# A graph layer's opening on one core: a fourth block of raw rows, later small loads, other places for the stores of gathered blocks, and two operands in PSUM

## The chip, the core and the metric

The kernel runs on one core of one Trainium2 chip. The metric is the device time of one execution in microseconds (us); the three runs of the kernel before have a median of 4114.34 us (4112.78 to 4116.98). The core has five engines with a queue of instructions each: TensorE (PE in the profile, with weight loads as PEld), VectorE (DVE), ScalarE (ACT), GpSimd (POOL) and SyncE (SP). DMAs are issued from the queues of SP and ACT, and POOL issues indirect DMAs, which gather rows by a list of indices. All engines issue in order and wait for each other through semaphores.

## The reference, cut to what matters

There are N = 12500 nodes with C = 96 features, and E = 412500 edges, sorted by destination. Every edge has four attributes.

```
def mlp(h, W, b, gamma, beta):
    h = relu(h @ W + b)
    mu, var = mean(h, axis=0), mean(square(h - mu), axis=0)
    return gamma * (h - mu) * rsqrt(var + EPS) + beta

node_feat = mlp(x, W_node, ...)                     # N rows
edge_feat = mlp(edge_attr, W_edge, ...)             # E rows
message   = mlp(concat([x[src], x[dst], edge_feat]), W_msg, ...)
agg       = segment_sum(message, dst, N)
out       = layernorm(x + agg + node_feat)
```

The first 96 rows of W_msg act on x[src], the next 96 on x[dst]. So the kernel computes two tables once, p = x @ W_msg[:96] and q = x @ W_msg[96:192], and a message needs one row of p and one row of q. Norms are over all edges or nodes, so the statistics of edge_feat must be known before any message.

## The kernel before, in words

**Units.** 128 edges are a tile, 4 tiles a group (512 edges), 4 groups a block. There are 202 blocks and 3223 tiles. For every tile POOL issues one indirect DMA that fetches 128 rows of p (function `gather`, line L172); that is the only way in which p's rows reach the messages. q's rows need no gather, because edges are sorted by destination: a window of 31 rows serves a group.

**The opening, in the order of the code.** SP and ACT load x transposed (`xp`, seven pieces, L95) and the indices. `tables` (L157 to L165) computes p and q in seven chunks of 14 x 128 rows: matmuls, copies into one of two `trow` buffers, and per chunk one store to `p_tab` and one to `q_tab`, which alternate between SP and ACT. A third chunk cannot reuse a buffer before the first one's two stores have landed.

Main messages can start only after the edge statistics, but gathers need not wait. The first 26 blocks (`SPILL`) are gathered into one of two `stage` buffers and stored to DRAM (`spill`, L183) by SP; later they are read back. This is the generator `blocks`: each `next(store)` puts 16 gathers into POOL's queue and one store into SP's queue at that place of the code. A gather of block b needs the store of block b-2 to have landed, because there are two buffers. Blocks below `RAW` = 3 are gathered from x itself instead of p_tab, so they need not wait for the tables; the function `convert` (L435 to L443) multiplies them by W_msg[:96] when they come back in the main loop.

After the tables SP loads a few small things (L196 to L199), 13 pieces of the edge weights (`wide`, `we`, L202 to L207), and `dsti`, the destinations (L211). VectorE subtracts each block's first node (`basei`, L215) to get `rel`, and finds whether all edges fit their windows (`worst`, `flag`, L219 to L229). `places` (L235 to L252) loads the destinations in another layout (`lin`), subtracts `first` (L245), squares (L248) and stores both to DRAM (`rel_d`), two parts at a time. `lin` reuses the memory of `dsti`, and `dsti` that of `trow`. `nodes` (L261 to L284) computes the node features and stores them in 13 pieces (`y_d`, L282). `edge_norm` (L297 to L338) reads all edge attributes in 26 chunks of eight blocks (`ea`, two buffers), with matmuls, ReLU and batch statistics on VectorE (L309); between its chunks stand further `next(store)`, by a rule of 100 stores to 73 x the chunk's number.

**The main loop.** POOL gathers the 176 other blocks into a ring of 21 group buffers (`pg`). For a group PE makes z (L464), VectorE adds z and pg into hs (L475), ACT applies ReLU, PE sums (L497), VectorE accumulates (L510, L511). The 26 stored blocks are mixed evenly among the others. A short last part adds the node part and normalises the rows.

**What sets the order.** Inside `manual_schedule` SP and POOL keep the order of the code; a planner sorts everything else, by the time at which it thinks an instruction ready. The tables and their `next(store)` are one such section, `places` to `edge_norm` another. The small loads, the weights and `dsti` stood between them, so that the planner moved the loads forward among the stores of the tables.

Of the kernel before, what the change touches and what calls it, by code (L numbers as in the profile page):

```python
# [11 lines left out]
F32 = mybir.dt.float32  # L12
I32 = mybir.dt.int32
AF = mybir.ActivationFunctionType
OP = mybir.AluOpType
AX = mybir.AxisListType
ET = mybir.EngineType
PSUM = bass.MemoryType.PSUM
DRAM = bass.MemoryType.DRAM

N, C, E, ED = 12500, 96, 412500, 4
EPS = 1e-5
P = 128
# [3 lines left out]
GT, GE, BG = 4, 512, 4  # L27
NT = -(-E // P)
NG = -(-NT // GT)
NBL = -(-NG // BG)  # L30
NTP, NGP = NBL * BG * GT, NBL * BG
EP = NGP * GE
EK = ED + 1
Q = 32
NS = 3
RW = 7
# [14 lines left out]

SPILL = 26 * BG
RING = 21
RAW = 3
SKEW = 8
HB, RB = 2, 3
CL, CE = 2, 2
# [16 lines left out]
def gnn(ctx, tc, t):  # L74
    nc = tc.nc
# [31 lines left out]
    wide = const.tile([P, P], F32, name="wide")  # L107
    we = const.tile([P, C + WN], F32, name="we")


    step = const.tile([BG, 3, WN], F32, name="step")
# [13 lines left out]
    base = const.tile([1, NBL], I32, name="base")  # L125
    mstat = const.tile([C, 2], F32, name="mstat")
    vec = const.tile([C, len(_VECS)], F32, name="vec")
    v = {name[7:]: vec[:, i:i + 1] for i, name in enumerate(_VECS)}
    w_node = const.tile([C, C], F32, name="w_node")
    b_msg = const.tile([1, C], F32, name="b_msg")  # L130
# [56 lines left out]
    store = blocks()  # L187
    with tc.manual_schedule(engines={ET.SP, ET.Pool}):
        with tc.tile_pool(name="win_w", bufs=1) as work, tc.tile_pool(name="win_ps", bufs=4, space=PSUM) as ps:
            for i, _ in enumerate(tables(work, ps)):  # L190
                if i in (2, 4):
                    next(store)

    zero = const.tile([64, C], F32, name="zero")
    nc.vector.memset(zero, 0.0)
    nc.sync.dma_start(vec, t["vecs"])  # L196
    nc.sync.dma_start(w_node, t["L0_gnn_W_node"])
    nc.sync.dma_start(b_msg, t["L0_gnn_b_msg"])
    nc.sync.dma_start(base, t["base"])  # L199
    for i in range(NS):  # L200
        k, n = Q * i, C - Q * i
        nc.sync.dma_start(wide[k:k + EK, :n], t["wb"][:, C - n:])  # L202
        nc.sync.dma_start(wide[k + EK:k + 2 * EK, n:], t["wb"][:, :P - n])
    for i in range(BG):
        nc.sync.dma_start(we[Q * i:Q * i + EK, :C], t["wb"])
    for i in range(3):
        nc.sync.dma_start(we[ED + i:P:Q, C:], step[:, i, :])  # L207

    with tc.tile_pool(name="win", bufs=1) as win, tc.tile_pool(name="win_ps", bufs=2, space=PSUM) as ps:
        dsti = win.tile([P, NGP, GT], I32, name="dsti")  # L210
        nc.sync.dma_start(dsti, t["dst"].rearrange("p (g t) -> p g t", t=GT))  # L211
        basei = win.tile([P, NBL], I32, name="basei")
        nc.sync.dma_start(basei, t["base"].to_broadcast([P, NBL]))
        by_block = "p (b g) t -> p b (g t)"
        nc.vector.tensor_tensor(rel.rearrange(by_block, g=BG), dsti.rearrange(by_block, g=BG),  # L215
                                basei.unsqueeze(2).to_broadcast([P, NBL, BG * GT]), op=OP.subtract)
        worst = win.tile([P, 2, BG], F32, name="worst")
        for k in range(BG):
            nc.vector.tensor_reduce(worst[:, 0, k:k + 1], rel[:, k:NG:BG, :], axis=AX.XY, op=OP.max)  # L219
            nc.vector.tensor_reduce(worst[:, 1, k:k + 1], rel[:, k:NG:BG, :], axis=AX.XY, op=OP.min)  # L220
        out = win.tile([P, 1], F32, name="out")
        nc.vector.tensor_sub(worst[:, 0, :], worst[:, 0, :], iota[:, :, WN - 1])
        nc.vector.tensor_sub(worst[:, 1, :], iota[:, :, 0], worst[:, 1, :])
        nc.vector.tensor_reduce(out, worst.rearrange("p a k -> p (a k)"), axis=AX.X, op=OP.max)
        po = ps.tile([1, P], F32, name="po", bufs=1)
        nc.tensor.transpose(po, out, ident)
        most = win.tile([1, 1], F32, name="most")
        nc.vector.tensor_reduce(most, po, axis=AX.X, op=OP.max)
        nc.vector.tensor_scalar(flag, most, 0.0, None, op0=OP.is_gt)  # L229

    def places():

        with tc.tile_pool(name="lin", bufs=2) as work, tc.tile_pool(name="lin1", bufs=1) as one:
            first = one.tile([P, RW], I32, name="first")
            nc.sync.dma_start(first, t["first"])  # L235
            rows = [r.rearrange("o (p g e) -> (o p) g e", g=RW, e=GE) for r in rel_d]
            parts = [slice(i, min(i + 2, RW)) for i in range(0, RW, 2)]
            lins = []
            for i in range(len(parts) + 1):
                if i < len(parts):  # L240
                    n = parts[i].stop - parts[i].start
                    lins.append(work.tile([P, n, GE], I32, name="lin"))
                    nc.sync.dma_start(lins[i], t["dlin"][:, parts[i], :])
                    rlin = work.tile([P, n, GE], F32, name="rlin")
                    nc.vector.tensor_tensor(rlin, lins[i], first[:, parts[i]].unsqueeze(2).to_broadcast([P, n, GE]),  # L245
                                            op=OP.subtract)
                    square = work.tile([P, n, GE], F32, name="square")
                    nc.scalar.activation(square, rlin, AF.Square)  # L248
                    lins[i] = (rlin, square)
                if i:  # L250
                    for r, x in zip(rows, lins[i - 1]):
                        nc.sync.dma_start(r[:, parts[i - 1], :], x)  # L252

    def nodes():

        with tc.tile_pool(name="nd", bufs=1) as one, tc.tile_pool(name="nd_ps", bufs=2, space=PSUM) as ps:
            stats = one.tile([C, -(-N // GE), 6], F32, name="nstats")
            for i, c in enumerate(range(0, N, GE)):
                n = min(GE, N - c)
                pn = ps.tile([C, GE], F32, name="pn", bufs=4)  # L260
                nc.tensor.matmul(pn[:, :n], w_node, xp[:, c:c + n], start=True, stop=True)  # L261
                nc.scalar.activation(agg[:C, c:c + n], pn[:, :n], AF.Relu, bias=v["b_node"], scale=1.0)
                nc.vector.bn_stats(stats[:, i, :], agg[:C, c:c + n])
            aggr = one.tile([C, 2], F32, name="naggr")
            nc.vector.bn_aggr(aggr, stats.rearrange("p a b -> p (a b)"))
            a_n, c_n = norm(aggr, v["g_node"], v["beta_node"], "node")
            for c in range(0, N, N // 10):
                x, y = agg[:C, c:c + N // 10], xp[:, c:c + N // 10]
                nc.vector.scalar_tensor_tensor(y, x, a_n, y, op0=OP.mult, op1=OP.add)
                nc.scalar.activation(y, y, AF.Identity, bias=c_n, scale=1.0)  # L270
            for i in range(0, NB, NBY):
                n = min(NBY, NB - i)
                py = ps.tile([P, 2, GE], F32, name="py0")
                for g in range(n):
                    nc.tensor.matmul(py[:, g // NBK, g % NBK * C:(g % NBK + 1) * C],  # L275
                                     xp[:, (i + g) * P:(i + g + 1) * P], center, start=True, stop=True)
                y0 = one.tile([P, 2, NBK * C], F32, name="y0s", bufs=2)
                if n == NBY:
                    nc.vector.tensor_copy(y0, py[:, :, :NBK * C])
                else:  # L280
                    nc.vector.tensor_copy(y0[:, 0, :n * C], py[:, 0, :n * C])
                nc.sync.dma_start(y0_d[i // NBY][:, :n * C], y0.rearrange("p a b -> p (a b)")[:, :n * C])  # L282
                yield
            nc.vector.memset(agg, 0.0)  # L284
# [55 lines left out]
    def fast(ring):  # L340
# [3 lines left out]
        with tc.manual_schedule(engines={ET.SP, ET.Pool}):  # L344
            nc.sync.dma_start(q_tab[:WM, :], zero[:WM])
            for r in range(WM + NN, WT, 64):
                n = min(64, WT - r)
                nc.sync.dma_start(q_tab[r:r + n, :], zero[:n])
            next(store)
            places()  # L350
            next(store)
            next(store)
            for i, _ in enumerate(nodes()):
                if i in (1, 5, 10):
                    next(store)
            xpool.close()
            n = 0
            for i, _ in enumerate(edge_norm()):
                if 73 * i >= 50 + 100 * n:
                    next(store, None)  # L360
                    n += 1
            for _ in store:
                pass
            got = {g: ahead_of(g) for g in range(SPILL, SPILL + RING)}
# [11 lines left out]
        with tc.tile_pool(name="fix", bufs=1) as fix, tc.tile_pool(name="msg", bufs=2) as work, \  # L376
# [138 lines left out]
            n, ahead = len(steps), SPILL + RING  # L515
# [202 lines left out]
    with tc.tile_pool(name="fin", bufs=2) as work, tc.tile_pool(name="fin_ps", bufs=2, space=PSUM) as ps:  # L718
# [14 lines left out]
        for i in range(0, NB, NBY):  # L733
            n = min(NBY, NB - i)
# [55 lines left out]
```

## Time and profile before

| what | us |
|---|---|
| median of three runs | 4114.34 |
| profiled execution, its own time | 4124.01 |
| its span | 4122.3 |
| first gather starts | 3.15 |
| first gather of block 5 starts | 122.08 |
| first gather into the ring starts | 555.65 |
| first hs (main loop) starts | 633.54 |
| last gather starts | 4066.01 |
| POOL busy, 3244 instructions | 3072.2 |
| PE busy, mean granted clock 0.728 | 2875.0 |
| DVE busy | 1245.9 |

A line of a timeline gives the start and the duration in us, the engine (a q behind it: its queue issues, for a DMA), the line of the kernel, the operation, what it writes and reads, and in brackets how long the engine sat idle before and what ended that. A line of the waits gives the total in us, how many times, and the longest.

### The profile page before, as it was taken

The page shows a single profiled execution, that of the slowest core. Times are in us where ns is not written, and L with a number is a line of the kernel's source. Part 1 is how long each engine was busy: PE and PEld are TensorE (multiplying, and loading weights), DVE is VectorE, ACT ScalarE, POOL GpSimd, SP SyncE. Part 2 cuts the span into 40 slices and gives each one's busy share as a digit, 9 for nine tenths or more (in the row PEclk, how much of TensorE's full clock was granted, in tenths as well). Part 3 has the DMA queues.
Part 4 walks back from the last instruction along what each step waited for, and adds up shares of the span by engine and source line. Part 5 has one row for each costly group of instructions (what it writes and reads, how often), then busy time and mean ns, then how long its engine had stood idle before and what let it go on. Part 6 is the DMA issues. An engine that isn't in the chain of part 4 may idle for free. (4 is left out here: it accounts for less than half of the span.)

```text
span 4122.3 us, 46288 instructions
## 1 busy us (share of the span) xinstructions
PE 2875.0 (70%) x16517; PEld 2372.3 (58%) x16517; DVE 1245.9 (30%) x2410; ACT 1035.6 (25%) x804; POOL 3072.2 (75%) x3244
## 2 busy tenths in 40 slices
PE   4699968776667766666576667766777667666666
PEld 4455537666556655655565556666666556555555
DVE  2599983222122222222122212221222122221223
ACT  1387753221112211111122111121211122211112
POOL 6777777777777777777777777777777777777775
PEclk7655558877677778778777777776777677878777
DMA  8555532222222222222222222222222222222224
GB/s 241 170 115 110 106 78 67 48 54 54 53 53 47 54 52 47 53 55 54 52 47 54 52 54 46 54 55 52 46 54 54 53 46 54 54 52 47 54 53 114
DMA packets 190373, 274.29 MB, mean 67 GB/s; under 512 B 121571, under 2 KB 121956, under 8 KB 189126
## 3 DMA queue, kind: packets, MB, share of 16 engines
q0 software_dynamic: 103136, 158.62, 18.4%
q1 hardware_dynamic: 71684, 99.14, 8.8%
q10 hardware_dynamic: 15312, 13.47, 1.2%
q8 instruction: 133, 2.18, 0.2%
q14 instruction: 108, 0.88, 0.1%
HBM read 227.55 MB, written 43.43 MB: 66 GB/s over the span
## 5 line engine op out<-in xcount | busy, mean ns | idle before, releaser
L172 POOL DMA_INDIRECT pg<-p_tab,src x2807 | 2654.7, 946 | 856.9 <-issue 766.0
L464 PE MATMUL z<-rhs,left 128*128 128x96 f32 x6446 | 1172.6, 341 | 1050.8 <-issue 613.3
L464 PEld LDWEIGHTS z<-rhs,left 128*128 128x128 f32 x6446 | 1063.0, 250 | 1312.7 <-issue 718.6
L475 DVE TENSOR_TENSOR hs<-z,pg 128x384 f32<-128x384 f32 x702 | 391.4, 557 | 2510.5 <-DMA pg<-p_tab,src 2199.7
L497 PE MATMUL pa<-h 128*97 128x128 f32 x6446 | 1112.4, 330 | 12.5 <-ACT h L482 9.0
L497 PEld LDWEIGHTS pa<-h 128*97 128x97 f32 x6446 | 989.7, 212 | 18.5 <-ACT h L482 15.2
L482 ACT ACTIVATE h<-hs 128x1536 f32<-128x1536 f32 x201 | 298.1, 1483 | 2018.3 <-DVE hs L475 2018.3
L457 ACT ACTIVATE left<-pr 127x2048 f32<-127x2048 f32 x202 | 378.4, 1873 | 716.8 <-PE pr L450 716.8
L172 POOL DMA_INDIRECT stage<-p_tab,src x368 | 352.8, 959 | 127.9 <-issue 107.7
L303 PE MATMUL pr<-ea,wide 10*128 10x512 f32 x1212 | 372.0, 1062 | 18.8 <-DMA ea<-in_ea 18.8
L309 DVE BATCH_NORM_STATS2 estats<-r 128x6 f32<-128x512 f32 x606 | 361.3, 676 | 25.5 <-ACT r L307 25.5
L307 ACT ACTIVATE r<-pr 128x1024 f32<-128x1024 f32 x303 | 293.1, 1024 | 141.8 <-PE pr L303 117.9
L303 PEld LDWEIGHTS pr<-ea,wide 10*128 10x128 f32 x1212 | 198.2, 319 | 191.3 <-ACT r L307 85.3
L450 PE MATMUL pr<-ea,we 7*127 7x512 f32 x1404 | 229.6, 725 | 12.8 <-DMA ea<-rel_d 12.8
L478 DVE TENSOR_TENSOR h<-rel,z 128x496 f32<-128x496 f32 x202 | 133.4, 660 | 0.0
L511 DVE TENSOR_TENSOR gram<-pa,gram 97x388 f32<-97x388 f32 x202 | 111.3, 551 | 0.0
L510 DVE TENSOR_TENSOR agg<-pa,agg 97x62 f32 x404 | 90.0, 223 | 36.8 <-PE pa L497 20.8
L475 DVE TENSOR_TENSOR hs<-z,pb 128x384 f32<-128x384 f32 x104 | 57.7, 555 | 114.7 <-PE z L464 114.7
L450 PEld LDWEIGHTS pr<-ea,we 7*127 7x127 f32 x1404 | 61.4, 205 | 43.2 <-issue 23.4
L172 POOL DMA_INDIRECT stage<-in_x,src_raw x48 | 45.6, 949 | 27.3 <-issue 10.7
L275 PE MATMUL py<-center,xp 96*128 96x96 f32 x196 | 42.8, 423 | 31.5 <-ACT xp L270 18.5
L275 PEld LDWEIGHTS py<-center,xp 96*128 96x128 f32 x196 | 42.0, 332 | 32.3 <-ACT xp L270 18.9
(113 smaller groups left out, 501.4 us busy)
## 6 DMA issues: line engine op xcount, KB each, us to landing
pg<-p_tab,src POOLq DMA_INDIRECT x2807
spill<-stage SPq DMA_DIRECT2D x26, 768.0 KB
pb<-spill SPq DMA_DIRECT2D x26, 768.0 KB
ea<-in_ea SPq DMA_DIRECT2D x75, 160.0 KB
rhs<-q_tab SPq DMA_DIRECT2D x202, 46.5 KB
ea<-in_ea SPq DMA_DIRECT2D x352, 20.0 KB
stage<-p_tab,src POOLq DMA_INDIRECT x368
y_d<-y0s SPq DMA_DIRECT2D x12, 384.0 KB
```

The lines of the kernel that those rows point to most:

```text
L172: nc.gpsimd.indirect_dma_start(out=pg[:, i, :], out_offset=None, in_=tab[:, :], in_offset=bass.IndirectOffsetOnAxis(ap=idx[:, k:k + 1], ax ...
L303: nc.tensor.matmul(pr[:, k % 2, :], wide[Q * i:Q * i + 2 * EK, :], ea[Q * i:Q * i + 2 * EK, b % J, :], start=True, stop=True)
L307: nc.scalar.activation(r, pr, AF.Relu)
L309: nc.vector.bn_stats(stats[:, (k - o) % NS, (k - o) // NS, :], r[:, 1 - o, :])
L450: nc.tensor.matmul(prs[s][:C + WN, i, :], we[Q * i:Q * i + EK + 2, :], block[s][Q * i:Q * i + EK + 2, :], start=True, stop=True)
L457: nc.scalar.activation(x[:C + WN, :n, :], pr[:C + WN, :n, :], AF.Relu)
L464: nc.tensor.matmul(zs[k][:, i, :], left[s % 2][:KR, g % BG, i * P:(i + 1) * P], rhs[:KR, s % RB, g % BG, :], start=True, stop=True)
L475: nc.vector.tensor_add(hs[:, i, :n, :], z[:, :n, :], pg[:, :n, :])
L478: nc.vector.tensor_tensor(h[:, :, :, C + 1:C + 1 + WN], rel[:, b:b + BG, :].unsqueeze(3).to_broadcast([P, BG, GT, WN]), nodes_of.unsqueeze ...
L482: nc.scalar.activation(h[:, :, :, :C], hs, AF.Relu)
L497: nc.tensor.matmul(pas[s][:, g % BG, :C + 1 + WN], h[:r, i, :C + 1], h[:r, i, :C + 1 + WN], start=i == 0, stop=i == n - 1)
L511: nc.vector.tensor_add(gram[:, :n, :], pa[:, :n, :C + 1], gram[:, :n, :])
```

## The change

`RAW` becomes 4. In `tables` blocks 0, 1 and 2 are put behind chunks 0, 2 and 5 (before: blocks 0 and 1 behind chunks 2 and 4, block 2 ahead of `places`). Four small loads get a fixed place behind the tables; the 13 loads of edge weights become a function that is called behind `places` and two blocks. `nodes` has its three blocks behind stores 2, 5 and 11 (before 2, 6 and 11). The subtraction at L215 takes the blocks' first nodes from PSUM, spread over the partitions by a matmul with a row of ones, instead of from SBUF, spread by a DMA; `places` keeps a copy of `first` in PSUM.

```
-RAW = 3
+RAW = 4
...
             for i, _ in enumerate(tables(work, ps)):
-                if i in (2, 4):
+                if i in (0, 2, 5):
                     next(store)
+            nc.sync.dma_start(vec, t["vecs"])
+            nc.sync.dma_start(w_node, t["L0_gnn_W_node"])
+            nc.sync.dma_start(b_msg, t["L0_gnn_b_msg"])
+            nc.sync.dma_start(base, t["base"])
...
-    nc.sync.dma_start(vec, t["vecs"])
-    nc.sync.dma_start(w_node, t["L0_gnn_W_node"])
-    nc.sync.dma_start(b_msg, t["L0_gnn_b_msg"])
-    nc.sync.dma_start(base, t["base"])
-    for i in range(NS):
-        k, n = Q * i, C - Q * i
-        nc.sync.dma_start(wide[k:k + EK, :n], t["wb"][:, C - n:])
...
+    def edge_weights():
+        for i in range(NS):
+            k, n = Q * i, C - Q * i
+            nc.sync.dma_start(wide[k:k + EK, :n], t["wb"][:, C - n:])
+            nc.sync.dma_start(wide[k + EK:k + 2 * EK, n:], t["wb"][:, :P - n])
+        for i in range(BG):
+            nc.sync.dma_start(we[Q * i:Q * i + EK, :C], t["wb"])
+        for i in range(3):
+            nc.sync.dma_start(we[ED + i:P:Q, C:], step[:, i, :])
...
         nc.sync.dma_start(dsti, t["dst"].rearrange("p (g t) -> p g t", t=GT))
-        basei = win.tile([P, NBL], I32, name="basei")
-        nc.sync.dma_start(basei, t["base"].to_broadcast([P, NBL]))
+        ones = win.tile([1, P], F32, name="ones")
+        nc.vector.memset(ones, 1.0)
+        basef = win.tile([1, NBL], F32, name="basef")
+        nc.vector.tensor_copy(basef, base)
+        pb = ps.tile([P, NBL], F32, name="pb", bufs=1)
+        nc.tensor.matmul(pb, ones, basef, start=True, stop=True)
...
-                                basei.unsqueeze(2).to_broadcast([P, NBL, BG * GT]), op=OP.subtract)
+                                pb.unsqueeze(2).to_broadcast([P, NBL, BG * GT]), op=OP.subtract)
...
-            first = one.tile([P, RW], I32, name="first")
-            nc.sync.dma_start(first, t["first"])
+            firsti = one.tile([P, RW], I32, name="firsti")
+            nc.sync.dma_start(firsti, t["first"])
+            first = ps.tile([P, RW], F32, name="first")
+            nc.vector.tensor_copy(first, firsti)
...
-            next(store)
             places()
             next(store)
             next(store)
+            edge_weights()
+            next(store)
             for i, _ in enumerate(nodes()):
-                if i in (1, 5, 10):
+                if i in (1, 4, 10):
                     next(store)
```

More of the change, by code (lines that the diff above doesn't have):

```diff
@@ L190, in gnn @@
             for i, _ in enumerate(tables(work, ps)):
-                if i in (2, 4):
+                if i in (0, 2, 5):
                     next(store)
+            nc.sync.dma_start(vec, t["vecs"])
+            nc.sync.dma_start(w_node, t["L0_gnn_W_node"])
+            nc.sync.dma_start(b_msg, t["L0_gnn_b_msg"])
+            nc.sync.dma_start(base, t["base"])
     zero = const.tile([64, C], F32, name="zero")
     nc.vector.memset(zero, 0.0)
-    nc.sync.dma_start(vec, t["vecs"])
-    nc.sync.dma_start(w_node, t["L0_gnn_W_node"])
-    nc.sync.dma_start(b_msg, t["L0_gnn_b_msg"])
-    nc.sync.dma_start(base, t["base"])
-    for i in range(NS):
-        k, n = Q * i, C - Q * i
-        nc.sync.dma_start(wide[k:k + EK, :n], t["wb"][:, C - n:])
[L203 to L207, printed above, removed]
+    def edge_weights():
[7 more added lines that the diff above has]
+            nc.sync.dma_start(we[ED + i:P:Q, C:], step[:, i, :])
     with tc.tile_pool(name="win", bufs=1) as win, tc.tile_pool(name="win_ps", bufs=2, space=PSUM) as ps:
@@ L231, in places @@
     def places():
-        with tc.tile_pool(name="lin", bufs=2) as work, tc.tile_pool(name="lin1", bufs=1) as one:
-            first = one.tile([P, RW], I32, name="first")
-            nc.sync.dma_start(first, t["first"])
+        with tc.tile_pool(name="lin", bufs=2) as work, tc.tile_pool(name="lin1", bufs=1) as one, \
+                tc.tile_pool(name="lin_ps", bufs=1, space=PSUM) as ps:
+            firsti = one.tile([P, RW], I32, name="firsti")
+            nc.sync.dma_start(firsti, t["first"])
+            first = ps.tile([P, RW], F32, name="first")
+            nc.vector.tensor_copy(first, firsti)
             rows = [r.rearrange("o (p g e) -> (o p) g e", g=RW, e=GE) for r in rel_d]
```

## Prediction

> **What bounds the kernel now.** I read the page first, then the waits of GpSimd, then the timelines of GpSimd and SyncE over the opening, and last the start of the main loop. The page's chain was no help: it reaches back only to 4077 us. The page's span, its engine row and the costliest group:
>
> ```profile
> span 4122.3 us, 46288 instructions
> PE 2875.0 (70%) x16517; PEld 2372.3 (58%) x16517; DVE 1245.9 (30%) x2410; ACT 1035.6 (25%) x804; POOL 3072.2 (75%) x3244
> L172 POOL DMA_INDIRECT pg<-p_tab,src x2807 | 2654.7, 946 | 856.9 <-issue 766.0
> ```
>
> POOL looks 75% busy, but between two gathers lie 0.30 us that the profile calls issue. The waits of POOL say how often it waited for something else:
>
> ```profile
> POOL pg L172 <- issue: 766.0, 2512, 0.3
> POOL pg L172 <- DMA pg<-p_tab,src: 82.1, 266, 1.3
> POOL stage L172 <- DMA spill<-stage: 9.7, 3, 5.6
> ```
>
> 766.0 over 2512 is 0.30 each, so a gather costs 0.95 + 0.30 = 1.25 us and POOL runs flat out. All 3223 take 4029 us. The first starts at 3.15 and the last at 4066.01, 4062.9 apart, so everything that ever held POOL adds up to some 35 us. That is the most that any change outside the gathers can win. From POOL's timeline (start, duration, line, and in brackets the idle time before), the holds of the opening:
>
> ```profile
> 24.50 0.95 POOL L172 DMA_INDIRECT stage<-in_x,src_raw  x1 [0.84 <-DMA stage<-in_x,src_raw]
> 54.91 0.94 POOL L172 DMA_INDIRECT stage<-in_x,src_raw  x1 [5.65 <-DMA spill<-stage]
> 75.85 0.95 POOL L172 DMA_INDIRECT stage<-p_tab,src  x1 [1.25 <-issue]
> 85.86 3.18 POOL L172 DMA_INDIRECT stage<-p_tab,src  x1 [0.30 <-issue]
> 122.08 0.95 POOL L172 DMA_INDIRECT stage<-p_tab,src  x1 [3.75 <-DMA spill<-stage]
> 555.65 0.95 POOL L172 DMA_INDIRECT pg<-p_tab,src  x1 [0.30 <-issue]
> ```
>
> 122.08 is gather 80, the first of block 5. Flat out from 3.15 it would start at 103.15; 18.9 us were lost, about 6.4 of them between 15 and 32 us (a gather waits for one eight earlier, beside the loads of xp), 5.35 at 54.91 (block 2 waits for block 0's store), 0.95 at 75.85 (p_tab), 2.2 at 85.86, 0.5 near 102, 3.45 at 122.08 (block 5 waits for block 3's store). SyncE's timeline shows why these stores are late:
>
> ```profile
> 34.05 0.40 SPq L165 DMA_DIRECT2D p_tab<-trow  x1
> 43.84 2.55 SPq L183 DMA_DIRECT2D spill<-stage  x1
> 55.20 2.66 SPq L183 DMA_DIRECT2D spill<-stage  x1
> 68.90 0.36 SPq L165 DMA_DIRECT2D p_tab<-trow  x1
> 76.02 0.36 SPq L211 DMA_DIRECT2D dsti<-in_dst  x1
> 97.12 0.81 SPq L243 DMA_DIRECT2D lin<-in_dlin  x2
> 116.44 0.32 SPq L252 DMA_DIRECT2D rel_d<-square  x1
> 117.06 4.96 SPq L183 DMA_DIRECT2D spill<-stage  x2
> ```
>
> Block 3's store stands behind places(), whose last store goes at 116.44. places() in turn stands behind the flag, that behind dsti, and that behind the last rows of the tables. This chain on SP is what I follow.
>
> **The change, part by part.** The sum is against the profiled execution (4124.01 us, span 4122.3), which is 9.7 us above the median of 4114.34; I carry differences over to the median.
>
> *Small loads moved* (13 of edge weights, 4 others). In front they made table stores wait: ScalarE's copy at 34.06 was held 12.41 us by "DMA wide<-in_wb", and the first p_tab store went at 34.05 though its last copy ended at 18.7. Now it can go at about 19. Yet SP meets block 0's store next and waits for its gathers (last one issued at 24.50, landed by 33). So block 0's store goes at some 34 instead of 43.84, and lands by 34 + 11 = 45 (old: 43.84 to 54.91). Block 2 wants the buffer at 49.6: the 5.35 us go, and gathers 32 to 47 run 5.35 us sooner, the last issued at 73.66 - 5.35 = 68.3. Behind places() the 13 loads cost SP 13 x 0.3 to 2.5 us (the rows of L202 to L207) before block 5's store, whose gathers need until about 143 anyway: hidden; uncovered, 4 to 30 us on SP.
>
> The Trainium skill's "DMA: Bandwidth & Descriptors", section "Queues, rings and completion order", has each engine consume one queue's ring in order; by it the store issued at 19 moves nothing until the xp loads ahead of it land near 31, so these 15 us of issue would be worth some 4. No part of my sum uses them.
>
> *Fourth raw block.* Gathers 48 to 63 read x, so block 3 waits for no p_tab: 0.95 us gone. A raw gather costs 949 ns against 946: nothing. Its convert in the main loop is one more of three (L435 to L443: 15 us of PE in the row at 650.6 to 665.2), and hidden, because VectorE there waits 2199.7 us for pg. Uncovered it is 15 us, once.
>
> *PSUM operands.* L215 (3.53 us from 84.69) and the L245 operations (1.23 us) stretch gathers beside them: 3.18 and 1.41 us instead of 0.95. The copy to `first`, the memset, the basef copy and one K=1 matmul are about 0.2 us each by VectorE's small rows, 0.4 by po's matmul (L226). Whether a PSUM operand frees POOL no row shows: bounds 0 and 2.7 us. The Trainium skill's "SBUF — State Buffer", section "Who interferes with whom", says two SBUF inputs contend with a GpSimd operation that reads SBUF and one does not, which would give the 2.7 us; it also infers that such operations spare descriptor writing, which the 3.18 us row contradicts. In the sum this is worth 0, because POOL now waits further on. `first` also takes a bank of PSUM until the last L245 (115.6 us), and may keep the nodes' matmuls (from 96.93) waiting.
>
> *The wait that collects all this.* Block 5 needs block 3's buffer. Gathers 48 to 79 would now be done 12.5 us sooner, block 5 wanting to start at 109.6. But its release follows SP's chain, and there block 2's store now stands ahead of the last p_tab store, and four small loads behind it:
> - block 2's gathers landed: 68.3 + 4.3 to 6.9 (block 4: 117.38 to 121.7; block 1: 48.32 to 55.2), I take 73.0;
> - p_tab's last store behind that 0.79 MB store: 5.0 to 7.1 us (117.06 to 122.08 for one such store; 68.90 to 76.02 for the two last table stores), I take 5.9, so 78.9 against 76.0 before; the four loads and the zero rows fit inside it;
> - dsti until L215: 8.67 before, with basei (0.43 us of issue) and a zero store behind it; 7.0 to 8.7, I take 7.4, so 86.3 against 84.69;
> - L215 to block 5: 122.08 - 84.69 = 37.4, less 0.9 for eight gathers fewer beside the places' 6 MB (0 to 1.5): 36.5.
>
> Block 5 starts at 122.8: **0.7 us later than before**, with all ends together 120.5 to 128.4. The holds that vanish at 54.91, 75.85, 85.86 and 102 come back as one wait of about 13 us. From there on POOL's order is unchanged.
>
> *Stores at other places.* Block 6 after y_d 2, 7 after y_d 5, 8 after y_d 11. Block 8's gathers land near 206, so y_d 12 and 13 and the first ea loads go at about 207 instead of 196 and 197, and in edge_norm every ea chunk now stands behind the store of the block after the one before. At its end three chunks instead of two follow the last gathered block (557.04): 24 x 0.594 = 14.3 us more VectorE (L309), so the main loop starts some 15 us later relative to POOL. What covers it: 21 buffers are 84 gathers, filled at 555.65 + 105 = 660.7, while the first hs was at 633.54: 27 us, of which 12 remain.
>
> Sum: +0.7, so 4114.34 + 0.7 = **4115.0 us**.
>
> **The rivals.**
> 1. *The new wait is short.* If places() ended by 104, block 5 would start at 109.6: -12.5, time 4101.8; half of it, 4108. For it: dsti needs only the c6 rows landed, and SP is less crowded. Against it: block 2 cannot land before 72.6, so SP's own order allows block 5 no earlier than 120.5.
> 2. *Slower: the ring fills before the main loop starts.* Place: the 85th pg gather. From 27 us of delay on, every us costs one. 15 are used; if PSUM's bank keeps the nodes' stage from 96.93 to 117 (20 us), and the stores do not hide it, the delay is 35: +8 to +9, time 4123. Against: y_d 12 waits for block 8's gathers anyway, which hides about 10 of the 20.
> 3. *SP held, no more.* SP waits for block 0 and 1 while later table rows stand ready, c5 and c6 slip, and all takes its late end: block 5 at 128.4, +6.3, time 4120.6.
>
> **How the numbers follow.** A difference under 0.2% (8.2 us) is what a measurement of this kernel can hardly tell from none. Chances: forecast 0.68, rival 1 0.13, rival 2 0.11, rival 3 0.08. Rival 1 mostly goes below 4106 (0.10), with tails of the forecast, whose later holds on the ea loads may shift by 3 us: faster 0.12; rival 2 and the tails of rival 3: slower 0.10; the rest, 0.78, the same. The range reaches from half-way into rival 1, 4105, to rival 2's price, 4123; forecast alone 4110 to 4120.
>
> **What would show it.** After: one wait of 10 to 16 us ahead of the first gather of block 5 for "spill<-stage", none at block 2; that gather at 120 to 128; p_tab's first store near 19; no gather of 3 us beside L215; the first hs some 15 us later; pg still waiting on issue only. Wrong if block 5 starts before 114, or pg gathers wait for hs.

## The result, and the profile after

The changed kernel takes 4121.01 us (median of 22 runs, 4116.90 to 4124.89). The kernel before, on the same chip, takes 4113.72 us (22 runs, 4109.92 to 4117.26). The ratio is 1.0017 with a 95% interval of 1.0011 to 1.0023: some 7 us more, inside the 0.2% that I called no change, though the interval's upper end reaches past it. The forecast was 4115.0, so 6 us are missing from it.

The profiled executions hide this. They took 4124.01 us before and 4123.96 after, because that of before lay 9.7 us above its median, and POOL's pace differs: from the first ring gather to the last, 2806 gathers later, it is 1.2510 us per gather before and 1.2483 after ((4066.01 - 555.65) / 2806 and (4065.09 - 562.40) / 2806), 7.7 us over the whole. No run shows the kernel to be the cause of those 7.7 us: the four edited kernels on an equal chip, below, lie between at 1.2496 to 1.2502, and the difference is there ahead of the ring too, where unheld gathers (numbers 110 to 416) follow each other at 1.2509 and 1.2484. So I take times from medians and only places and waits from the profiles.

The page after, its span, engine row and costliest group:

```profile
span 4122.2 us, 46400 instructions
PE 2811.1 (68%) x16567; PEld 2316.5 (56%) x16567; DVE 1251.1 (30%) x2417; ACT 1038.0 (25%) x808; POOL 3063.1 (74%) x3244
L172 POOL DMA_INDIRECT pg<-p_tab,src x2807 | 2648.4, 944 | 855.5 <-issue 789.7
```

The bound is the same: one gather after the other, 0.94 + 0.30 us. So everything is again decided by what holds POOL, and the waits of POOL after (total, times, longest) say what that is:

```profile
POOL pg L172 <- DMA pg<-p_tab,src: 59.1, 194, 0.3
POOL stage L172 <- DMA stage<-p_tab,src: 22.1, 19, 3.7
POOL stage L172 <- DMA spill<-stage: 12.8, 1, 12.8
```

Waits of 0.3 us are the ordinary gap between two gathers under another name. The last two rows are real. Three waits for a store of gathered blocks (9.7 us before) have become one of 12.8. And the waits for an earlier gather's landing have grown from 16.2 us in 16 waits to 22.1 in 19, the longest from 2.4 to 3.7. POOL's timeline after (start, duration, in brackets the idle time before) shows the places:

```profile
49.74 0.94 POOL L172 DMA_INDIRECT stage<-in_x,src_raw  x1 [0.30 <-issue]
87.19 0.94 POOL L172 DMA_INDIRECT stage<-in_x,src_raw  x1 [0.30 <-issue]
89.69 0.95 POOL L172 DMA_INDIRECT stage<-p_tab,src  x1 [0.30 <-issue]
108.41 0.94 POOL L172 DMA_INDIRECT stage<-p_tab,src  x1 [0.30 <-issue]
122.13 0.94 POOL L172 DMA_INDIRECT stage<-p_tab,src  x1 [12.78 <-DMA spill<-stage]
363.53 0.94 POOL L172 DMA_INDIRECT stage<-p_tab,src  x1 [1.28 <-DMA stage<-p_tab,src]
370.63 0.94 POOL L172 DMA_INDIRECT stage<-p_tab,src  x1 [3.66 <-DMA stage<-p_tab,src]
562.40 0.94 POOL L172 DMA_INDIRECT pg<-p_tab,src  x1 [0.30 <-issue]
```

Block 2 (49.74) waits for nothing, nor does the first gather from p_tab (89.69), and the gather at 87.19, beside the subtraction L221 (L215 of before), takes 0.94 us and not 3.18. All that was won stands at 108.41, the last gather of block 4, and all of it goes in the wait that follows: block 5 starts at 122.13, against 122.08 before. The two rows near 365 are the other kind of wait. By gather number, the time lost against 1.2503 us per gather (a pace between those of the two profiles) is:

| gathers | before | after |
|---|---|---|
| 0 to 80 | 18.9 | 19.0 |
| 80 to 208 | 3.9 | 5.3 |
| 208 to 416 | 9.5 | 14.9 |
| first ring gather (number 416) starts | 555.65 | 562.40 |

So in these two profiles the opening costs the same, and the difference of 6.75 us arises behind it, nearly all of it while the edge attributes are read. SyncE's timeline after, first the chain that I followed:

```profile
22.77 0.40 SPq L165 DMA_DIRECT2D p_tab<-trow  x1
33.16 0.33 SPq L183 DMA_DIRECT2D spill<-stage  x1
71.55 0.33 SPq L183 DMA_DIRECT2D spill<-stage  x1
71.99 0.83 SPq L165 DMA_DIRECT2D p_tab<-trow  x1
79.76 0.36 SPq L213 DMA_DIRECT2D dsti<-in_dst  x1
116.22 0.32 SPq L261 DMA_DIRECT2D rel_d<-square  x1
116.84 1.49 SPq L183 DMA_DIRECT2D spill<-stage  x2
```

and then a place where gathers were held, from the same view, with the answering place of before in a second fence:

```profile
351.46 0.35 SPq L183 DMA_DIRECT2D spill<-stage  x1
351.98 5.39 SPq L306 DMA_DIRECT2D ea<-in_ea  x6
```

```profile
370.27 0.35 SPq L183 DMA_DIRECT2D spill<-stage  x1
370.78 11.47 SPq L297 DMA_DIRECT2D ea<-in_ea  x6
```

After, the six loads of two chunks (160 KB each) go out within 5.39 us, right behind a store of 0.79 MB. Gathers issued just behind them land late, and a gather waits for the one eight earlier: that of 370.63 waited for the one issued at 356.32, which so took some 14 us to land. Before, at 370.78, the six take 11.47 us, and POOL loses 0.2 us behind them. Of the pairs of chunks in edge_norm, five go out within 5.4 to 6.9 us after, three before. The short ones are followed by 2.2 to 4.3 us of holds each, the three of 9.5 to 11.5 us by 0.2 to 0.6, and the first pair of before, 13.59 us long, by 1.4. A single chunk right behind a store is followed by 0 to 0.8 us, and one that goes over 1 us behind it by none. That is the suspicion, theory A, that the experiments had to test.

### The profile page after: what moved, and what is told of

Its sections match the earlier page's. It is cut to its first block, busy times and chain, and to the rows that moved or that the text cites. A ratio compares the mean times of both kernels' runs of the same rounds, so it can differ in the third digit from the quotient of the medians.

```text
span 4122.2 us, 46400 instructions
## 1 busy us (share of the span) xinstructions
PE 2811.1 (68%) x16567; PEld 2316.5 (56%) x16567; DVE 1251.1 (30%) x2417; ACT 1038.0 (25%) x808; POOL 3063.1 (74%) x3244
## 5 line engine op out<-in xcount | busy, mean ns | idle before, releaser
L172 POOL DMA_INDIRECT pg<-p_tab,src x2807 | 2648.4, 944 | 855.5 <-issue 789.7
L474 PE MATMUL z<-rhs,left 128*128 128x96 f32 x6446 | 1122.8, 331 | 1093.1 <-issue 650.2
L474 PEld LDWEIGHTS z<-rhs,left 128*128 128x128 f32 x6446 | 1016.2, 240 | 1349.5 <-issue 763.4
L507 PE MATMUL pa<-h 128*97 128x128 f32 x6446 | 1085.7, 324 | 16.1 <-ACT h L492 13.3
L507 PEld LDWEIGHTS pa<-h 128*97 128x97 f32 x6446 | 960.9, 207 | 23.5 <-ACT h L492 20.1
L172 POOL DMA_INDIRECT stage<-p_tab,src x352 | 335.1, 952 | 137.6 <-issue 102.7
L312 PEld LDWEIGHTS pr<-ea,wide 10*128 10x128 f32 x1212 | 207.4, 320 | 193.7 <-issue 88.3
L172 POOL DMA_INDIRECT stage<-in_x,src_raw x64 | 60.5, 946 | 27.1 <-issue 16.2
L157 PE MATMUL pt<-w_msg,xp 96*128 96x192 f32 x196 | 41.9, 384 | 27.8 <-DVE trow L163 18.4
```

Source lines behind the costliest of these rows:

```text
L172: nc.gpsimd.indirect_dma_start(out=pg[:, i, :], out_offset=None, in_=tab[:, :], in_offset=bass.IndirectOffsetOnAxis(ap=idx[:, k:k + 1], ax ...
L312: nc.tensor.matmul(pr[:, k % 2, :], wide[Q * i:Q * i + 2 * EK, :], ea[Q * i:Q * i + 2 * EK, b % J, :], start=True, stop=True)
L474: nc.tensor.matmul(zs[k][:, i, :], left[s % 2][:KR, g % BG, i * P:(i + 1) * P], rhs[:KR, s % RB, g % BG, :], start=True, stop=True)
L507: nc.tensor.matmul(pas[s][:, g % BG, :C + 1 + WN], h[:r, i, :C + 1], h[:r, i, :C + 1 + WN], start=i == 0, stop=i == n - 1)
```

## The experiments

Theory A: the 7 us come from the place of the gathered blocks' stores in edge_norm. Because nine blocks instead of eight are issued before it, each chunk of edge attributes stands behind the store of one block later; SP then finds both `ea` buffers empty more often, sends two chunks back to back, and they hold the gathers. Theory B: the loss is in the opening (the one long wait), or spread, and the place in edge_norm is worth nothing. The first four runs were on a chip where the kernel before takes 4116.68 us. The changed kernel itself was not run there, so it is compared with them by its ratio to the kernel before, 1.0017.

**e1: the rule of edge_norm shifted back by one block, in the changed kernel.**

```
-            n = 0
+            n = 1
```

> The changed kernel, but in edge_norm every gathered block's store goes one step of the rule later (n starts at 1 instead of 0), so that ea chunks stand behind the same blocks' stores as before the change. Theory A (the 7 us were lost in edge_norm, where two chunks' loads now go back to back behind a store and late gathers hold POOL): the holds of POOL from the first ea load to the first ring gather fall from 15 to about 9.5 us, the first hs is some 12 us earlier, time 4114 to 4116. Theory B (they were lost earlier, by the nodes' stage that now starts 18 us later, or by the wait at block 5): time 4120 to 4122.

Measured: 4113.87 us (4111.87 to 4115.62), ratio to the kernel before 0.9993 (0.9984 to 1.0002). Its timeline of SP at the same place:

```profile
368.57 0.35 SPq L183 DMA_DIRECT2D spill<-stage  x1
370.03 15.26 SPq L306 DMA_DIRECT2D ea<-in_ea  x6
```

The six loads now take 15.26 us, since SP waits for a buffer between the two chunks, and no gather behind them is held. The time lost in gathers 208 to 416 falls from 14.9 to 1.0 us, the waits for earlier gathers from 22.1 to 6.2, and the ring starts at 547.44 instead of 562.40. Block 5 still starts at 120.83. The holds fall further than the 9.5 us that I expected by theory A. This one number takes back the whole loss, and theory B falls.

**e2: block 3's store ahead of places(), in the changed kernel; the rule as changed.**

```
+            next(store)
             places()
             next(store)
-            next(store)
             edge_weights()
```

> The changed kernel, but block 3's store stands on SyncE ahead of places() instead of behind it. My account of the change (everything that vanished from POOL's opening came back as one wait of 12.5 us at block 5, for this store): the wait is gone, block 5 starts at about 109.7 instead of 122.1, and all of it reaches the end: time about 4108.5. Rival (another wait takes its place within the next blocks, since their stores stand behind places and the nodes): block 5 early, but 4118 or more.

Measured: 4107.49 us (4105.89 to 4111.22), ratio 0.9980 (0.9970 to 0.9989). SP and POOL of this kernel:

```profile
78.55 0.36 SPq L213 DMA_DIRECT2D dsti<-in_dst  x1
89.63 0.36 SPq L183 DMA_DIRECT2D spill<-stage  x1
97.75 0.81 SPq L252 DMA_DIRECT2D lin<-in_dlin  x2
```

```profile
107.13 0.95 POOL L172 DMA_INDIRECT stage<-p_tab,src  x1 [0.30 <-issue]
108.38 0.94 POOL L172 DMA_INDIRECT stage<-p_tab,src  x1 [0.30 <-issue]
```

108.38 is the first gather of block 5, and it waits for nothing. The store goes at 89.63, while SP would only have waited for the places' first operands. The opening now loses 5.3 us instead of 19.0, and the kernel is some 16 us below the changed one (1.0017 x 4116.68 = 4123.7, less 4107.5). So the gains that the change made in the opening were real, and were lost to the order of two lines of code. They are not all of the 16 us: the ring starts 20.8 us sooner (541.61), of which 13.7 come from the opening and 7.1 from fewer holds behind it, because only three pairs of chunks go out within 5.9 to 6.4 us here, with the rule of the changed kernel. 10.4 us in gathers 208 to 416 remain.

**e3: both edits, in the changed kernel.**

```
+            next(store)
             places()
             next(store)
-            next(store)
             edge_weights()
...
-            n = 0
+            n = 1
```

> Both edits together, block 3's store ahead of places() and edge_norm's stores one step later. If the two losses are separate they add: 4121 - 12.5 - 6 = about 4102.5, which is under both kernels. If they share a cause (a POOL that is earlier finds the ea loads earlier too and is held longer): 4106 to 4110.

Measured: 4103.65 us (4102.53 to 4108.71), ratio 0.9970 (0.9961 to 0.9981). This beats both kernels.

```profile
108.02 0.94 POOL L172 DMA_INDIRECT stage<-p_tab,src  x1 [0.30 <-issue]
537.73 0.94 POOL L172 DMA_INDIRECT pg<-p_tab,src  x1 [0.30 <-issue]
```

The opening loses 4.9 us, gathers 208 to 416 lose 0.1. The ring starts 24.7 us sooner than in the changed kernel. What is left is 9.5 us in gathers 80 to 208, of which 6.7 lie at three gathers between 216.9 and 237.6. The first two of them (4.6 us) fit the same pattern: the very first six loads of edge attributes find both buffers empty and go out from 202.57 to 205.02. That was not tried apart.

**e4: the rule shifted the other way in the kernel before.** If theory A holds, this alone must make the kernel before slower.

```
-            n = 0
+            n = -1
```

> The kernel before, with only edge_norm's stores one step earlier (n starts at -1), which is where the change puts them; all else as before. Theory A: the loss of the change shows without the change, holds up by 4 to 6 us, first hs some 12 us later, time 4118 to 4120. Theory B: no difference, 4113 to 4115.

Measured: 4120.83 us (4117.96 to 4122.83), ratio 1.0010 (1.0001 to 1.0019), so 4 us slower, and at the lower end of the interval nothing. Gathers 80 to 208 lose 5.8 us (3.9 before), 208 to 416 lose 10.5 (9.5). SP's timeline shows the pattern of the changed kernel: five pairs of chunks go out within 5.9 to 6.7 us, where the kernel before has three, and each is followed by 2.4 to 2.7 us of holds. The sign is as theory A has it; the size is less than the 10 us by which e1 moved the changed kernel, and the two profiles alone show only 1 us of it at the start of the ring (556.70 against 555.65, the latter from an execution 9.7 us above its kernel's median).

So e1 and e4 show that the place of the stores in edge_norm changes how long gathers are held. That it does so through the two chunks sent back to back is read from the six profiles: ahead of the ring's start all 16 pairs that go out within 5.4 to 6.9 us are followed by 2.2 to 4.3 us of holds, and the 18 that take 9.5 to 16.2 us by at most 1.5 (those of e1 and e3 by at most 0.4, also where, as at 328.18 and 428.60 in e1, they stand right behind a store). The run made to test the loads by themselves, e8, decides nothing.

**The other eight runs** were made to price the parts of the change singly. They came to chips on which TensorE at times stands still for over 20 us, and the kernel before takes 5300 to 5314 us; so they answer a different question from the one that was asked, and only comparisons among themselves are used. This is the changed kernel there (run e11), TensorE's timeline:

```profile
37.77 9.25 PE L157 MATMUL pt<-w_msg,xp 96*128 96x192 f32 x36 [11.10 <-DVE trow L163]
70.28 5.12 PE L157 MATMUL pt<-w_msg,xp 96*128 96x192 f32 x16 [23.26 <-issue]
96.24 12.28 PE L157 MATMUL pt<-w_msg,xp 96*128 96x192 f32 x56 [13.58 <-DVE trow L163]
```

and its waits of POOL:

```profile
POOL pg L172 <- DVE hs L485: 784.5, 133, 132.6
POOL stage L172 <- DMA spill<-stage: 230.1, 12, 32.9
POOL pg L172 <- DVE agg L520: 193.0, 54, 4.9
```

At 47.02 TensorE stops in the middle of the tables for 23.26 us, with nothing to wait for that the profile shows. It is not alone: VectorE stands still for 25.30 us, put down to issue as well, until its copy at 69.27, whose end TensorE's restart follows by 0.05 us, and ScalarE for 30.05 us until 80.47. Which of them holds the others isn't settled. The tables' last rows go at 109.07 instead of 71.99, block 5 starts at 161.13, and in the main loop the ring is full: 784.5 us of waits for hs. POOL is not the bound there.

**e11: the changed kernel, nothing edited, on such a chip.**

> The changed kernel once more, with nothing edited, beside the kernel before on one chip: the base that the four runs with TensorE's pauses lack. If those pauses are there again (kernel before near 5300 us, tables ready only near 110 us), the late tables set block 5 at 155 to 162, and the ratio to the kernel before tells what is common to the four runs; by the theory that operands in SBUF, four blocks per load and the place of the small loads change little there, it is 1.006 to 1.012. Rival: one of these edits was itself the loss, and the ratio is under 1.003. If the pauses are not there, ratio 1.0011 to 1.0023 as before, block 5 at 121 to 123.

Measured: 5354.75 us against 5299.90, ratio 1.0116 (1.0087 to 1.0146). There the change is a clear loss, and it is common to most of the edited kernels, as expected of this run.

**e5 and e12: three blocks of raw rows instead of four** (the same kernel, twice).

```
-RAW = 4
+RAW = 3
```

> The changed kernel with RAW = 3 again, so block 3's gathers must wait for p_tab. My account says that the fourth raw block wins nothing as long as block 5 waits for block 3's store: the gathers of block 3 start some 8 us later (79 instead of 69.7), the wait at block 5 shrinks by the same, block 5 starts at 121 to 123, and the time is that of the change within 3 us, 4119 to 4125. Rival: it buys its 8 us, and the time without it is 4127 to 4132.

> The changed kernel with three blocks of raw rows instead of four, all else as changed. Without the pauses of TensorE: block 3 (gather 48, wanted at about 68) waits for the last rows of p_tab until about 78, but block 5 waits for block 3's store behind the places anyway, so block 5 starts at 121 to 124 and the time stays within 2 us of the changed kernel (ratio to the kernel before 1.0012 to 1.0024). Rival: the wait is not absorbed, block 3's gathers land later than SyncE reaches their store, block 5 starts 5 to 10 us later and the kernel takes 1.003 to 1.004 times the kernel before. With the pauses: block 3 waits some 25 us for p_tab instead of block 4 some 30, and the ratio is 0.006 or so below that of the unedited changed kernel in this same call, as in the earlier run.

Measured: 5335.65 us and 1.0035 (1.0013 to 1.0058); 5317.73 us and 1.0040 (1.0019 to 1.0061). The second is 37 us less than e11 on the same chip. In these two profiles block 5 starts 19.8 us sooner (141.29 against 161.13), since the tables' last rows go at 85.12; the ring starts 29.1 us sooner, and the last gather 36.1. So there the fourth raw block is most of the loss. How it makes the tables later is not settled: their matmuls are the same, and the standstills come and go with no wait to explain them. The 7 us that are added in the main loop fit the converting of one more block, which I had priced at 15 us where nothing hides it; they are not shown to be that. What the fourth block is worth on a chip without these pauses was not measured.

**e6 and e10: block bases and first nodes in SBUF again, loaded by DMA** (the same kernel, twice).

```
-        pb = ps.tile([P, NBL], F32, name="pb", bufs=1)
-        nc.tensor.matmul(pb, ones, basef, start=True, stop=True)
+        basei = win.tile([P, NBL], I32, name="basei")
+        nc.sync.dma_start(basei, t["base"].to_broadcast([P, NBL]))
...
-            first = ps.tile([P, RW], F32, name="first")
-            nc.vector.tensor_copy(first, firsti)
+            first = one.tile([P, RW], I32, name="first")
```

> The changed kernel with the block bases and the first nodes in SBUF again (the DMA that spreads base, no matmul, no PSUM tile first). The gather beside the subtraction should take 3.2 us again instead of 0.95, which the wait at block 5 swallows; the nodes' matmuls should start near 99 instead of 115.6, since no bank is held. Time as the change's, 4118 to 4124. If the later nodes' stage is what costs the 7 us: 4113 to 4116.

> The changed kernel with block bases and first nodes as int32 in SBUF again, loaded by DMA as before; all else as changed. My prediction's step: a gather beside the subtraction from dsti takes about 3.2 us instead of 0.95 again, but GpSimd waits for block 3's store later on anyway, so the time stays within 2 us of the changed kernel (ratio to the kernel before 1.0012 to 1.0022) and block 5 stays at 121.5 to 123.5; without the bank that the first nodes hold, the nodes' matmuls start near 99 instead of 115.6, which the end doesn't show. Rival: the bank that is held delays the ea loads and so all that follows; then this kernel is 5 us or more faster than the changed one, ratio below 1.0005.

Measured: 5375.56 us and 1.0111 (1.0082 to 1.0140); 5355.44 us and 1.0110 (1.0091 to 1.0129), against 1.0116 for e11: the same time. But the local effect is plain. The subtraction runs from 127.11 to 130.65 in e10, and POOL beside it:

```profile
127.09 0.94 POOL L172 DMA_INDIRECT stage<-p_tab,src  x1 [0.30 <-issue]
128.34 3.13 POOL L172 DMA_INDIRECT stage<-p_tab,src  x1 [0.30 <-issue]
131.77 0.95 POOL L172 DMA_INDIRECT stage<-p_tab,src  x1 [0.30 <-issue]
```

In e11, with one operand in PSUM, it runs from 126.44 to 129.96, and POOL beside it:

```profile
127.01 0.94 POOL L172 DMA_INDIRECT stage<-p_tab,src  x1 [0.30 <-issue]
128.25 0.94 POOL L172 DMA_INDIRECT stage<-p_tab,src  x1 [0.30 <-issue]
129.50 0.94 POOL L172 DMA_INDIRECT stage<-p_tab,src  x1 [0.30 <-issue]
```

So the edit frees 2.2 us of POOL, and here, as in the changed kernel on a chip without pauses, it is lost to the next wait. It also turns the operand from int32 into fp32, but the type alone does not free POOL: beside L269 of the kernel before, whose two tensors in SBUF are both fp32, ten gathers take 1.12 to 1.20 us instead of 0.95. The nodes' matmuls start at 139.35 in e10 and at 155.02 in e11: the bank that `first` holds keeps them some 15 us, and the time does not show that either.

**e7: the edits of e3 and of e6 together.**

> The kernel with block 3's store ahead of places() and edge_norm's stores one step later, and with both operands in SBUF again. There no wait at block 5 swallows a held gather any more, so block 5 should start some 2.5 us later than with PSUM (110.6 against 108.0) and the time rise by about 2.5 us. If the operand's place does not matter to POOL: no difference, the gather beside the subtraction at 0.95 us.

Measured: 5345.86 us, ratio 1.0052 (1.0031 to 1.0073), against 1.0111 for e6 on the same chip; block 5 starts at 142.40 instead of 160.52. The two edits of order are worth 0.6% here, on a chip with another bound (without pauses 0.5%, 0.9970 against 1.0017). Where the 0.6% arise the profiles do not show: at the ring's start the gain is gone (794.24 against 783.31), and the profiled execution of e7 is the slowest of its 11. Gather 72, beside the subtraction, was held 2.33 us; whether that counts where POOL is the bound was not measured.

**e8: four blocks instead of eight per load of edge attributes.**

```
-J = 8
+J = 4
...
-                if 73 * i >= 50 + 100 * n:
+                if 73 * i >= 100 + 200 * n:
```

> The changed kernel with edge attributes loaded in chunks of four blocks instead of eight (J = 4, two buffers of half the size, the rule of the stores scaled so that they stand at the same blocks). Theory A (gathers are held when the loads of two chunks of 0.48 MB each go back to back behind a store): such a burst is 0.48 MB at most, and the holds between the first ea load and the ring fall from 15 to 20 us to under 8; time 4110 to 4114, unless edge_norm itself now starves and the ring fills. Theory B (each store of a block holds POOL, whatever the loads): holds and time as in the change, 4119 to 4123.

Measured: 5356.93 us, ratio 1.0074 (1.0049 to 1.0100), which overlaps e11's interval. With POOL waiting up to 27.6 us for stores of gathered blocks, the holds that this was to take away cannot be seen. It decides nothing.

**e9: the 13 loads of edge weights ahead of the tables' stores again.**

> The changed kernel with the 13 loads of edge weights back ahead of the tables' stores; all else as changed. The step of my prediction on the small loads says: they hold the first rows of p_tab, which then go at about 31 to 34 instead of 22.8, block 0's store behind them goes at 41 to 44 instead of 33.2, block 2 (gather 32) waits about 4 to 5.5 for it, and block 2's store, the rest of the tables, the flag and the places all follow on SyncE's queue, so that block 5 starts 4 to 6 us later than 122.1, at 126 to 128, and the kernel takes 3 to 6 us more than the changed one: 1.0024 to 1.0033 times the kernel before. Rival: the small loads cost issue only, the tables have slack behind block 2's gathers, block 5 starts at 121 to 123, and the ratio stays at 1.0013 to 1.0022.

Measured: 5361.06 us, ratio 1.0115 (1.0089 to 1.0142); block 5 starts at 160.88 against 161.13 in e11. The first rows of p_tab went at 32.03 (21.93 in e11), as expected, but behind the standstill that follows (23.6 us of TensorE) nothing of it is left at block 5. Its price without pauses stays open.

## Why the prediction came out as it did, step by step

**POOL flat out:** right where it was predicted (855.5 us of idle time ahead of 2807 ring gathers, 789.7 of it in plain 0.30 us gaps), and wrong on the chips with pauses.

**The four small holds of the opening go:** right. No wait at block 2, none for p_tab, 0.94 us beside L221, and no stretched gather beside the places. Block 0's store was forecast for 34 and went at 33.16; block 2's gathers landed by 71.55 (forecast 73.0). p_tab's first store was forecast for 19 and went at 22.77: its rows were ready earlier, but SyncE's waits put 4.6 us ahead of it down to a load of xp.

**They come back as one wait at block 5:** right, and closely. `dsti`, whose memory the last rows of p_tab must have left, went at 79.76 (78.9), `dsti` to L221 took 7.18 us (7.4), L221 started at 86.94 (86.3), from there to block 5 went 35.19 us (36.5), and block 5 started at 122.13 (122.8), after a wait of 12.78 us (13). e2 is the test of the cause: with block 3's store taken out from behind the places the wait is gone.

**Small loads:** the weights took SP from 118.77 to 127.10 and were hidden ahead of block 5's store at 143.47, as forecast. The section "Queues, rings and completion order" of the Trainium skill's "DMA: Bandwidth & Descriptors" has each DMA engine take one queue's descriptors in order, and the prediction's estimate from it made an earlier issue behind the xp loads worth little. The trace agrees, though no run tests it by itself: the first p_tab store went 11.3 us sooner (22.77 for 34.05), but the copy that waited for it started 2.9 us sooner (ScalarE, 37.79 for 40.67).

**PSUM operands, worth 0 between bounds of 0 and 2.7 us:** right as far as the runs go: e10 and e11 show that the one gather is freed and the time is not. They are from the chips with pauses; without pauses the operand was not taken back. The section "Who interferes with whom" of the Trainium skill's "SBUF — State Buffer" has the rule that two SBUF inputs contend with a GpSimd operation that reads SBUF, and one does not; 3.13 against 0.94 us for a gather beside the subtraction agrees. The prediction also took the row of 3.18 us to contradict what that section infers about descriptor writing; but a gather reads its list of indices from SBUF, so that row falls under the rule and does not test the inference. The guess that `first` would hold a bank until 115.6 was right as well: the nodes' matmuls started at 115.63 instead of 96.93, at no cost to the end.

**The main loop some 15 us later relative to POOL, 12 us of slack left:** right. From the first ring gather to the first hs went 77.9 us before (633.54 - 555.65) and 91.7 after (654.07 - 562.40), 13.8 more; the tightest ring buffer of the first turns came free 11.8 us ahead of its gather, and none was waited for.

**"From there on POOL's order is unchanged":** this is the step that failed, and with it the term of the sum behind block 5, which I had put at nothing. I moved the stores in edge_norm, saw that each chunk would stand behind the store of one block later, and priced only VectorE's later end. That the same move decides whether two chunks are loaded back to back, and that such loads hold gathers, I had left as a tail of 3 us. In its place stand the holds of gathers 80 to 416: 20.2 us after against 13.5 before in the profiles, and by the medians 10 us that e1 wins back with that one number. The mechanism stood in the trace of before: 16 waits for "stage<-p_tab,src", 16.2 us in all, with 1.6 to 2.1 us at one gather behind each pair of chunks that took 6 to 7 us. I counted them into the 35 us and never asked what made them. That the measured time still lies in my range, 4105 to 4123, is luck: it is above the 4110 to 4120 of the forecast alone, and the range reached further up for rival 2, a ring that fills, which did not happen.

**The rivals.** The short wait did not come, for the reason given against it; e2 shows what it would have been worth, 4107.5 where I had 4101.8 to 4108. The ring did not fill on this chip, and SP was not held to the late end of its range: block 5 started at 122.13, not at 128.4.

## What to carry to other kernels

When stores or loads change places in a queue that is issued in order, follow the queue to the end of the stage: what the loads now stand behind decides how many go out back to back, and here the engine that waits for gathers issued just behind them paid for it. Where a change removes several small waits ahead of one common gate, look for the store that keeps the gate shut and move it ahead of the long work in its queue; here that, with the loads spread out again, turned a loss of 0.17% into a gain of 0.30%. Price small waits that recur as a group, since their sum can exceed the one large wait that catches the eye.

## What the runs showed of the hardware that I had not expected

- Loads of 160 KB, six within 5.4 to 6.9 us behind a store of 0.79 MB, are followed by holds of the indirect gathers of 2.2 to 4.3 us in all 16 cases of six profiles; the same six over 13.7 to 15.3 us by at most 0.4 (the pairs of e1 between 271 and 442 us).
- One and the same kernel takes 4114 us on one chip and 5300 to 5314 on others. In e11 TensorE has 24 idle stretches of over 8 us that the profile puts down to issue, the longest 23.26 and all together 225 us, where the profile of before has one of 8.0 (mean granted clock 0.649 in e11, 0.728 in the profile before). The change is 0.17% slower on the first chip and 1.16% on the second. What makes the engines stand still, no run tells.
- POOL's pace for the same gathers differs by 0.2% between the profiled executions of before and after (1.2510 and 1.2483 us), 7.7 us over the ring, as much as the whole effect looked for here. No run shows why.
